# Two edge-attention layers on a graph: the prologue's order, the last three superchunks of a layer, and products added in pairs

## The chip, the cores and the metric

The kernel runs on one core of a Trainium2 chip. The metric is the time of one execution on the device in microseconds. One execution was also taken by the profiler; its page and its trace are what is read here.

## The reference

A graph has N = 6250 nodes with 256 features and E = 200,000 edges, sorted by their destination. The node features are normalised (layer norm), cut at zero, and go through two layers of graph attention; the result is added to the input. Cut to what matters (self loops with the mean of a node's edge features are added inside):

```python
h = jnp.maximum(_layernorm(x), 0.0)
def gat(x, s, d, ea, Wg, a_s, a_d, Wge, a_e, b, n, heads, f):
    hx, he = (x @ Wg).reshape(n, heads, f), (ea @ Wge).reshape(-1, heads, f)
    al = leaky_relu((hx * a_s).sum(-1)[s] + (hx * a_d).sum(-1)[d] + (he * a_e).sum(-1), 0.2)
    al = jnp.exp(al - segment_max(al, d, n)[d])
    al = al / segment_sum(al, d, n)[d]
    return segment_sum(hx[s] * al[:, :, None], d, n).reshape(n, -1) + b
te = relu(edge_attr @ We + be) * jnp.exp(x @ Wo + bo)[src][:, None]     # per layer
x1 = relu(gat(h, ..., te, 4 heads of 64) + h)
x2 = gat(x1, ..., te, 1 head of 256) + x1
out = x + x2 + h
```

## The kernel before, in words

**Tiles.** The edges are cut into 1563 chunks of 128 and these into 66 superchunks: 64 of 24 chunks, one of 14 and one of 13 (`cuts`). Each layer goes once over all superchunks, so there are 132 steps; step k is superchunk k of layer 0 for k below 66, and superchunk k - 66 of layer 1 after that. `st` holds the tiles of a step.

**The node table.** `prologue` loads x, normalises 49 tiles of 128 nodes (statistics L266 to L296, on VectorE or, for some groups, with their Newton steps on POOL; normalising L310), transposes them (L316), multiplies by the weights (L431), adds the bias (L435) and stores the rows as table T of layer 0 in DRAM. The same is done for 24 tiles of x rows gathered by source (`first_rows`, an indirect DMA each, issued by POOL at L250), which stay in the buffer G0 and so make the gathers of step 0 unnecessary. Index work of later superchunks (`index_group`) and folding the attention vectors into the weights (`fold`, `fold_e`) are woven in, one piece per tile.

**A step.** `edges` writes out the order by hand: each engine takes its instructions in the order in which the code issues them. For step k the loop issues the gathers of step k+1 (`gather` L874: one indirect DMA for each chunk, by POOL's queue, from T into one of three buffers G), the rest of the attention logits of step k (`logits`, `ends`, `links`, `maxima`), work for step k+1 (`spread`, `parts`, `rphase1`, `blocks`, `rphase2`, `adst`: edge features, and the nodes' terms brought to the edges), then `scale` (L1171: G times the weights), `carried`, `sums` (L1183: TensorE adds the scaled rows up by destination, with one-hot matrices S from `onehots` L1003), and `evict` (L1188: ScalarE copies the sums out of PSUM). `finish` of the step before (`merge`, L1204 to L1219 and what follows: self loop, division, bias, the next layer's table row) stands between `onehots` and `evict`; `rows1`, `rows2` and `rows3` make and store the rows of the nodes that are done. Superchunk s covers the nodes of a window of 112 that begins at its first destination; `nodes` loads their rows into one of five buffers `tw`.

**POOL's wait.** The gathers of a step go into a buffer that the sums of an earlier step have read, so they wait for these.

**The end of a layer.** `ending(st, nx, ...)` takes the last two superchunks together (k=64 and 65, k=130 and 131): the sums of the first are split in three with the other's work between them. At the end of layer 0 it also issues the gathers of step 66 (`after`), whose sources may lie in rows of layer 1's table that are not yet stored. The rows of the last window are therefore left out, and `add_last` (L842 to L852) adds them to the gathered rows of step 66 afterwards: 24 products of a one-hot matrix with the last 128 table rows, each followed by VectorE's addition of one chunk.

**Index data.** `index_group` fills, for a group of four superchunks, `loc`, `fpen`, `lpen`, `isl` and `pen`. `pen` is the penalty that cuts the scans of `ends` at the chunks' borders; for the four heads of layer 0 it is held in four copies (ScalarE copies three times at L604).

**Checks.** A few VectorE operations on the index data write flags into `bad`; the tile `wg`'s columns for the attention terms come from `fold`, those for the edge features from `fold_e`.

Of the kernel before, what the change touches and what calls it, by code (L numbers as in the profile page):

```python
# [31 lines left out]
P = 128  # L32
# [47 lines left out]
class Kernel:  # L80
# [32 lines left out]
    def consts(self, wp):  # L113
# [4 lines left out]
        self.wg, row, wpk = [], [], []  # L118
        self.ones = cp.tile([P, 1], F32, name="ones")
        nc.gpsimd.memset(self.ones, 1.0)  # L120
        self.bias, self.webd, self.be, wge = [], [], [], []
        for L in self.L:
            q = (nc.scalar, nc.sync)[L.l]
            wg = cp.tile([P, 2, L.MW], F32, name=f"wg{L.l}")
            q.dma_start(wg, a[f"wg{L.l}"].rearrange("(k p) m -> p k m", p=P))
            r = wp.tile([P, 3, D], F32, name=f"row{L.l}", bufs=1)
# [9 lines left out]
            e = wp.tile([P, D], F32, name=f"wge{L.l}", bufs=1)  # L136
# [34 lines left out]
        def fold(L):  # L171

            H = L.H
            for k in range(2):
                for j, c0 in ((0, L.p), (1, L.ad)):
                    t = wp.tile([P, D], F32, name="wtmp", bufs=4)
                    V.tensor_mul(t, self.wg[L.l][:, k, 0:D], row[L.l][:, j, :])
                    yield
                    V.tensor_reduce(self.wg[L.l][:, k, c0:c0 + H], t.rearrange("p (h f) -> p h f", h=H),
                                    axis=AX.X, op=OP.add)  # L180
                    yield

        def fold_e(L):

            H = L.H
            wea, we1 = self.wea[L.l]
            t = wp.tile([P, D], F32, name="wtmp", bufs=4)
            V.tensor_mul(t, wge[L.l], row[L.l][:, 2, :])
            yield
            V.tensor_reduce(we1, t.rearrange("p (h f) -> p h f", h=H), axis=AX.X, op=OP.add)  # L190
            yield
            for j in range(2):
                r = slice(j * PH, (j + 1) * PH)
                V.tensor_copy(wea[r, 32 * j:32 * j + H], we1[r, :])
            yield

        def later():
            yield from fold_e(self.L[0])
            yield from fold(self.L[1])
            yield from fold_e(self.L[1])  # L200

        return fold(self.L[0]), later()

    def prologue(self):
# [7 lines left out]
        with ExitStack() as c:  # L212
# [22 lines left out]
            for i in range(28):  # L235
                nc.tensor.matmul(warm[:, i % 2, :], self.ident, self.ident, start=True, stop=True)
# [19 lines left out]
            for _ in range(8):  # L256
                next(rows0, None)

            def stats(g):

                n, x = len(groups[g]), xs[g]
                st = wp.tile([P, GT, 6], F32, name="st", bufs=2)
                mv = wp.tile([P, GT, 2], F32, name="mv", bufs=3)
                s = wp.tile([P, 3, GT], F32, name="sc", bufs=3)
# [92 lines left out]
            for k in range(-3, len(tiles) + 1):  # L357
# [27 lines left out]
                if k >= 4:  # L385
# [19 lines left out]
    def fixed_rows(self):  # L405
# [18 lines left out]
        for i in range(2):  # L424
            self.trow1.append(cp.tile([P, 2 * L1.TW], F32, name=f"t1row{i}"))
            nc.gpsimd.memset(self.trow1[i][:, L1.TW + D:], 0.0)

# [9 lines left out]
    def indices(self, wp):  # L437
# [75 lines left out]
        chk = wp.tile([1, 9, NS + 1], F32, name="chk", bufs=1)  # L513
        V.memset(chk, 0.0)
        V.tensor_scalar(chk[:, 0, :NS], ll[0:1, :], float(M - 1), None, op0=OP.is_gt)
        V.tensor_sub(qd[0:1], qlast[0:1], qbase[0:1])
        V.tensor_scalar(chk[:, 5:9, :NS], qd[0:1], 31.0, None, op0=OP.is_gt)
        nb = wp.tile([1, NS + 1], F32, name="nb", bufs=1)
# [7 lines left out]
        V.tensor_tensor(chk[:, 3, :NS], sc0[0:1, 0, :], sc0[0:1, 2, :], op=OP.is_lt)  # L526
# [6 lines left out]
        self.before = cp.tile([P, NS], F32, name="before")  # L533
        V.tensor_copy(self.before, dpv)
        yield

    def index_tiles(self):
# [12 lines left out]
        self.pen = cp.tile([P, 4 * NCH + 1], BF, name="pen")  # L550
# [12 lines left out]
    def index_group(self, g, pool, di):  # L563
# [30 lines left out]
        pv = self.pen[:, 4 * o:4 * (o + w)].rearrange("p (s h c) -> p s h c", h=4, c=c)  # L594
# [5 lines left out]
        V.tensor_scalar(pv[:, :, 0, :], t3, 1.0, -BIG, op0=OP.min, op1=OP.mult)  # L600
        V.memset(self.pen[:, 4 * (o + w):4 * (o + w) + 1], -BIG)
        yield
        for h in range(1, 4):
            nc.scalar.activation(pv[:, :, h, :], pv[:, :, 0, :], AF.Copy)  # L604
            yield
# [11 lines left out]
    def edges(self, ctx):  # L617
# [13 lines left out]
        self.tws = [self.np_.tile([P, self.L[0].TW + D], F32, name=f"tw{i}", bufs=1) for i in range(5)]  # L631
        for t in self.tws:
            nc.vector.memset(t, 0.0)
# [11 lines left out]
        self.onehots(steps[0])  # L645
        self.edge_rows(steps[0])
# [3 lines left out]
        for k, st in enumerate(steps):  # L650
            nx = steps[k + 1] if k + 1 < len(steps) else None
            if st["s"] + 1 == self.NS:
                continue
# [4 lines left out]
            left = self.groups[self.ahead][0] - 2 - k if self.ahead < len(self.groups) else 99  # L658
# [3 lines left out]
            if st["s"] + 2 == self.NS:  # L662
                self.ending(st, nx, pv, late, steps[k + 2] if k + 2 < len(steps) else None)
# [35 lines left out]
            self.index_on(left)  # L699
            if k + 6 == self.NS:  # L700
# [12 lines left out]
    def ending(self, st, nx, pv, late, after):  # L713

        nc, k = self.nc, st["k"]
        self.load_lb(k + 3)
        self.gather(nx)
        for q in () if after else (st, nx):
# [3 lines left out]
        drain(self.logits(st))  # L722
        self.ends(st)
        self.spread(nx)
        self.parts(nx)
        y = self.rphase1(nx)
        next(y)
        self.links(st)
        if late:
            self.rows2(late)  # L730
        self.blocks(nx)
        if after:
            drain(self.finish(pv))
            self.rows3(late)
            self.rows1(pv)
            self.rows2(pv)
        drain(y)
        self.load_ea(k + 2)
        self.rphase2(nx)
        self.adst(nx)  # L740
        drain(self.maxima(st))
        if after:
            self.rows3(pv)
            self.gather(after)
            self.nodes(after)
            late = pv = None
        drain(self.scale(st))
        self.carried(st)
        c, h = nx["C"], st["C"] // 3
        self.sums(st, (0, h))  # L750
        self.edge_rows(nx)
        drain(self.logits(nx))
        self.ends(nx)
        self.sums(st, (h, 2 * h))
        self.onehots(nx)
        self.links(nx)
        self.sums(st, (2 * h, st["C"]))
        self.load_fl(k + 2)
        drain(self.maxima(nx))
        self.evict(st)  # L760
        y = self.rphase1(after) if after else iter(())
        next(y, None)
        drain(self.scale(nx, cuts=(1, 1 + c // 2, c)))
        drain(self.scale(nx, cuts=(0, 1)))
        if after:
            self.load_srow(after)
        self.carried(nx)
        self.sums(nx, (1, c), (0, 1))
        if late:
            self.rows3(late)  # L770
        if pv:
            drain(self.finish(pv))
            self.rows1(pv)
            self.rows2(pv)
            if not after:
                self.rows3(pv)
        f = self.finish(st)
        while after and "hw" not in st:
            next(f)
        if not after:  # L780
            drain(f)
            self.rows3(st)
        self.evict(nx)
        drain(f)
        drain(y)
        self.rows1(st)
        self.rows2(st)
        f = self.finish(nx)
        while after and "hw" not in nx:
            next(f)  # L790
        if after:
            self.rows3(st)
        drain(f)
        self.rows1(nx)
        self.rows2(nx)
        self.rows3(nx)
# [45 lines left out]
    def add_last(self, st):  # L842
# [5 lines left out]
        y = self.ps_y.tile([P, 1024], F32, name="y")  # L848
        for i in range(c):
            h = y[:, 512 * (i % 2):512 * (i % 2) + L.TW]  # L850
            nc.tensor.matmul(h, st["O"][:, i, :], st["last"], start=True, stop=True)
            V.tensor_add(G[:, i, 0:L.TW], G[:, i, 0:L.TW], h)  # L852
# [96 lines left out]
    def rphase1(self, st):  # L949
# [3 lines left out]
        c = st["C"]  # L953
# [98 lines left out]
    def logits(self, st):  # L1052
# [15 lines left out]
        n, p0 = H * c, 4 * o  # L1068
# [4 lines left out]
        V.tensor_tensor_scan(f, self.pen[:, p0:p0 + n], al[:, :n], -BIG, op0=OP.add, op1=OP.max)  # L1073
        yield
        V.tensor_tensor_scan(b[:, ::-1], self.pen[:, p0 + 1:p0 + n + 1][:, ::-1], al[:, :n][:, ::-1], -BIG,
# [469 lines left out]
```

## Time and profile before

| | |
|---|---|
| time before | 4817.07 us, median of 3 runs (4813.92 to 4823.6) |
| profiled execution | 4800.02 us |
| its span, first to last instruction | 4798.2 us |
| mean granted TensorE clock | 0.732 |
| busy: PE, VectorE, ScalarE, POOL | 3203.7, 2901.0, 520.2, 3011.0 us |
| first evict (k=0), first evict of layer 1 (k=66), last DMA's start | 213.2, 2623.7, 4786.9 us |

In the lines of the profile PE is TensorE's matmul, PEld its weight load, DVE VectorE, ACT ScalarE, POOL GpSimd, SP SyncE, which issues most plain DMAs. A line of the timeline has the start in us from the beginning of the span, the busy time in us, the engine, the line of the kernel, the operation, output and input tiles with their shapes, how many such instructions were put together, and in brackets the idle time of the engine just before and what ended it. A group's line (part 5 of the page) has the total busy time in us and the mean of one in ns, then the engine's idle time ahead of these instructions and its chief releaser; "issue" is time in which the engine waited for nothing that the profile shows, "remote" an event that could not be put down to an instruction.

### The profile page before, as it was taken

The numbers are of one execution on the slowest core, as the hardware profiler recorded it, in microseconds if no ns is written. First come the engines' busy times: TensorE is split into PE (matmuls) and PEld (weight loads), VectorE is DVE, ScalarE is ACT, GpSimd is POOL, SyncE is SP. The second block draws the span as 40 slices with busy tenths as digits, with TensorE's granted clock in tenths as the row PEclk, the third lists the DMA queues.
The fourth block names the chain that finished last, engine by engine and source line by source line (L and its number), as shares of the span: only waits on it lengthen the run. The fifth ranks groups of instructions, "written<-read, shape, count | busy, mean of one in ns | idle before, by whom it ended". The sixth has DMA issues, their size and how long they took to land. (4 is left out here: it accounts for less than half of the span.)

```text
span 4798.2 us, 35104 instructions
## 1 busy us (share of the span) xinstructions
PE 3203.7 (67%) x9964; PEld 1948.6 (41%) x9964; DVE 2901.0 (60%) x6782; ACT 520.2 (11%) x1152; POOL 3011.0 (63%) x3249
## 2 busy tenths in 40 slices
PE   7556766767767766767765666666666666666666
PEld 5334444444444444444442333333333433333334
DVE  6556766666766666666664555555455556455556
ACT  4111111111111111111110000000000000000000
POOL 5446666666666666666644666666666666666664
PEclk8676777776777777777775777777767777777777
DMA  6334444444444444444433444444444444444442
GB/s 218 93 104 119 128 130 119 129 131 119 130 127 122 128 128 126 124 126 127 126 108 92 126 118 117 124 120 124 116 124 126 118 116 125 119 124 117 124 125 69
DMA packets 240006, 585.82 MB, mean 122 GB/s; under 512 B 64201, under 2 KB 96655, under 8 KB 239609
## 3 DMA queue, kind: packets, MB, share of 16 engines
q0 software_dynamic: 150144, 422.75, 33.6%
q1 hardware_dynamic: 89243, 160.09, 10.2%
q8 instruction: 80, 1.31, 0.1%
q14 instruction: 123, 1.01, 0.1%
q10 hardware_dynamic: 416, 0.67, 0.0%
HBM read 544.42 MB, written 38.94 MB: 122 GB/s over the span
## 5 line engine op out<-in xcount | busy, mean ns | idle before, releaser
L874 POOL DMA_INDIRECT G<-T,src x3078 | 2937.8, 954 | 1679.3 <-issue 889.1
L1183 PE MATMUL u<-G,S 128*128 128x270 f32 (+1 forms) x6252 | 1648.0, 417 | 737.7 <-issue 588.3
L1183 PEld LDWEIGHTS u<-G,S 128*128 128x128 f32 x6252 | 1257.7, 203 | 1066.7 <-issue 643.0
L958 PE MATMUL y<-ea,webd 64*128 64x384 f32 (+1 forms) x1056 | 709.6, 795 | 326.8 <-issue 293.1
L1171 DVE TENSOR_TENSOR G<-G,kps 128x6144 f32<-128x6144 f32 (+1 forms) x137 | 853.0, 6230 | 0.0
L1096 DVE TENSOR_TENSOR_SCAN cl<-fl,cl,lf 4x129 f32<-4x129 f32 (+1 forms) x130 | 61.1, 470 | 898.5 <-remote 598.6
L958 PEld LDWEIGHTS y<-ea,webd 64*128 64x128 f32 x1056 | 281.4, 289 | 605.0 <-issue 540.2
L972 PE MATMUL zad<-R,wea 128*64 128x384 f32 (+1 forms) x1056 | 447.3, 764 | 10.2 <-ACT R L963 7.3
L1003 DVE TENSOR_TENSOR S<-kps,loc 128x3072 f32<-128x3072 f32 x132 | 437.5, 3315 | 4.5
L963 ACT ACTIVATE R<-y,webd 128x768 f32<-128x768 f32 x260 | 233.2, 897 | 649.8 <-PE y L958 293.8
L972 PEld LDWEIGHTS zad<-R,wea 128*64 128x64 f32 x1056 | 149.8, 197 | 309.5 <-issue 246.9
L1188 ACT ACTIVATE U<-u 128x270 f32<-128x270 f32 (+1 forms) x132 | 52.0, 394 | 1852.8 <-remote 1004.5
L1046 DVE STREAM_TRANSPOSE rt<-zad 128x768 f32<-128x768 f32 (+1 forms) x130 | 124.6, 959 | 15.9 <-issue 10.7
L1018 PE MATMUL zad<-a,Q 128*128 128x12 bf16 (+1 forms) x132 | 23.9, 181 | 163.4 <-issue 99.6
L431 PE MATMUL fin<-wg,h1T 128*128 128x260 f32 x264 | 119.5, 599 | 1.5 <-ACT h1T L1278 1.5
L987 DVE TENSOR_TENSOR lb<-lb,kps 128x1536 bf16<-128x1536 bf16 (+1 forms) x68 | 113.5, 1669 | 0.0
L1086 PE MATMUL lf<-ident,fb 128*36 128x128 f32 (+1 forms) x132 | 45.8, 347 | 98.6 <-issue 69.2
L431 PE MATMUL ps<-wg,hT 128*128 128x266 f32 x292 | 88.3, 429 | 28.4 <-ACT hT L318 17.8
L1103 PE MATMUL lf<-ident,cl 36*128 36x36 f32 (+1 forms) x132 | 35.4, 269 | 95.9 <-DVE cl L1098 95.8
L1270 DVE TENSOR_TENSOR t1row<-t1row,fb 128x256 f32<-128x256 f32 x66 | 28.2, 427 | 112.5 <-remote 60.4
L1103 PEld LDWEIGHTS lf<-ident,cl 36*128 36x128 f32 (+1 forms) x132 | 25.3, 192 | 168.9 <-DVE cl L1098 148.7
L1018 PEld LDWEIGHTS <-Q 128*128 128x128 bf16 x132 | 14.3, 108 | 190.7 <-issue 108.1
(202 smaller groups left out, 2248.4 us busy)
## 6 DMA issues: line engine op xcount, KB each, us to landing
G<-T,src POOLq DMA_INDIRECT x3078
ea<-in_ea_dram SPq DMA_DIRECT2D x64, 768.0 KB
lb<-locrow SPq DMA_DIRECT2D x64, 384.0 KB
T<-t1row SPq DMA_DIRECT2D x66, 227.5 KB
tw<-T SPq DMA_DIRECT2D x66, 225.8 KB
tw<-T SPq DMA_DIRECT2D x66, 117.2 KB
tw<-in_x_dram SPq DMA_DIRECT2D x66, 112.0 KB
part<-t1row SPq DMA_DIRECT2D x64, 113.8 KB
```

The source lines that it names most:

```text
L431: self.nc.tensor.matmul(ps[:, :L.MW], hT[:, k, :], self.wg[L.l][:, k, :], start=(k == 0), stop=(k == 1))
L874: nc.gpsimd.indirect_dma_start(out=G[:, c, 0:L.TW], out_offset=None, in_=rows, in_offset=bass.IndirectOffsetOnAxis(ap=idx[:, c:c + 1], axi ...
L958: nc.tensor.matmul(y[:, o], self.webd[l][r, :], ea[r, w], start=True, stop=True)
L963: nc.scalar.activation(R[:, i, :32 * c].rearrange("p (b n) -> p b n", b=2), y.rearrange("p (b n) -> p b n", b=2)[:, :, :16 * c], AF.Relu, ...
L972: nc.tensor.matmul(st["zad"][i * PH:(i + 1) * PH, o], self.wea[l][0], R[:, i, w], start=True, stop=False)
L987: V.tensor_tensor(lb[:, :, :n], lb[:, :, :n], self.k_part.unsqueeze(2).to_broadcast([P, i, n]), op=OP.is_equal)
L1003: nc.vector.tensor_tensor(st["S"][:, c0:c1, :], self.k_iota.unsqueeze(1).to_broadcast(w), self.loc[:, o + c0:o + c1].unsqueeze(2).to_broad ...
L1046: V.transpose(rv[:, :32 * c].rearrange("p (b n) -> p b n", b=2), z.rearrange("p (b n) -> p b n", b=2)[:, :, :16 * c])
L1096: V.tensor_tensor_scan(cl[:H, :], fl[:H, :], lf[:H, 0:P + 1], init, op0=OP.add, op1=OP.max)
L1103: nc.tensor.transpose(pc, cl[:n, 0:P], self.ident[0:n, 0:n])
L1171: nc.vector.tensor_tensor(v, v, pw[:, c0:c1, :].unsqueeze(3) .to_broadcast([P, c1 - c0, H, L.F]), op=OP.mult)
L1183: nc.tensor.matmul(st["u"][:, :L.W], S[:, i, :], G[:, i, 0:L.W], start=(j == 0), stop=(j == c - 1))
```

## The change

1. **Prologue.** 14 of the gathers of `first_rows` are issued ahead of the tiles (8 before); the others come one every third tile from the 15th (one every tile from the fifth before). 34 dummy matmuls on the identity come first (28 before), and 8 and 3 more at tiles 1 and 6. The statistics of the 24 gathered tiles are made in two groups of 6 and 18 (four of 6). `fold` of layer 1 moves to `edges`, behind the one-hot matrices of step 0; `fold_e` of layer 1 and the flags (`checks`) move into the loop, two pieces per step from k=6. The `tw` buffers are four, not five, and POOL zeroes them behind the 14 gathers.
2. **Penalty.** `pen` is held once; a layer-0 step copies it for its four heads into `pen4` at the start of `rphase1`, on ScalarE.
3. **Ending.** `ending(a, b, c, ...)` takes the last three superchunks (24, 14 and 13 chunks). The sums of a are split into a half and two quarters, with work of b and c between them. The step ahead of it is finished right behind its own evict.
4. **`add_last`.** Two products go to the two halves of one PSUM tile, taken in turn from two pools, and one addition takes both.

The diff, cut to these parts:

```diff
@@ prologue
-            for i in range(28):
+            for i in range(34):
                 nc.tensor.matmul(warm[:, i % 2, :], self.ident, self.ident, start=True, stop=True)
...
-            for _ in range(8):
+            for _ in range(14):
                 next(rows0, None)
+            for t in self.tws:
+                nc.gpsimd.memset(t, 0.0)
...
-            for i in range(0, CX, 6):
-                xs[len(groups)] = G0[:, i:min(i + 6, CX), 0:D]
-                groups.append(list(range(NT + i, NT + min(i + 6, CX))))
+            for i, e in ((0, min(6, CX)), (6, CX)):
+                if i < e:
+                    xs[len(groups)] = G0[:, i:e, 0:D]
+                    groups.append(list(range(NT + i, NT + e)))
...
-                    if q > g:
+                    if q > (g if k >= NT - 4 else min(g, g0)):
...
+                if k in (1, 6):
+                    idle(9 - k)
...
-                if k >= 4:
+                if k >= 14 and k % 3 == 0:
                     next(rows0, None)
@@ consts
-        def later():
-            yield from fold_e(self.L[0])
-            yield from fold(self.L[1])
-            yield from fold_e(self.L[1])
-
-        return fold(self.L[0]), later()
+        self.late, self.soon = fold_e(self.L[1]), fold(self.L[1])
+        return fold(self.L[0]), fold_e(self.L[0])
@@ index_group
-        for h in range(1, 4):
-            nc.scalar.activation(pv[:, :, h, :], pv[:, :, 0, :], AF.Copy)
-            yield
@@ rphase1
+        if H > 1:
+            st["pen"] = pen = self.pen4[st["k"] % 2]
+            nc.scalar.activation(pen[:, :H * c].rearrange("p (h c) -> p h c", c=c),
+                                 self.pen[:, o:o + c].unsqueeze(1).to_broadcast([P, H, c]), AF.Copy)
@@ nodes
-        tw = self.tws[st["k"] % 5]
+        tw = self.tws[st["k"] % 4]
@@ edges
         self.onehots(steps[0])
+        drain(self.soon)
         self.edge_rows(steps[0])
...
-            if st["s"] + 1 == self.NS:
+            if st["s"] + 2 >= self.NS:
                 continue
...
-            if st["s"] + 2 == self.NS:
-                self.ending(st, nx, pv, late, steps[k + 2] if k + 2 < len(steps) else None)
+            if st["s"] + 3 == self.NS:
+                self.ending(st, *steps[k + 1:k + 3], pv, late, steps[k + 3] if k + 3 < len(steps) else None)
...
             self.index_on(left)
+            if k >= 6:
+                next(self.late, None)
+                next(self.late, None)
+            if st["s"] + 4 == self.NS:
+                drain(self.finish(st))
@@ ending (the order of a's sums and the work between them)
+        self.gather(b)
+        self.gather(c)
...
+        drain(self.scale(a))
+        self.carried(a)
+        n = a["C"]
+        self.sums(a, (0, n // 2))
+        self.rows3(late)
+        self.edge_rows(b)
+        self.onehots(b)
+        drain(self.logits(b))
+        self.ends(b)
+        self.rows1(pv)
+        self.spread(c)
+        self.parts(c)
+        self.sums(a, (n // 2, n - n // 4))
+        self.links(b)
+        self.sums(a, (n - n // 4, n))
...
+        self.evict(a)
...
+        if after:
+            drain(self.finish(a))
+            self.rows1(a)
+            self.rows2(a)
+        drain(self.scale(b))
+        if after:
+            self.rows3(a)
+            self.gather(after)
+            self.nodes(after)
...
@@ add_last
-        y = self.ps_y.tile([P, 1024], F32, name="y")
-        for i in range(c):
-            h = y[:, 512 * (i % 2):512 * (i % 2) + L.TW]
-            nc.tensor.matmul(h, st["O"][:, i, :], st["last"], start=True, stop=True)
-            V.tensor_add(G[:, i, 0:L.TW], G[:, i, 0:L.TW], h)
+        for i in range(0, c, 2):
+            y = self.ps_y.tile([P, 1024], F32, name="y") if i % 4 else self.ps_1.tile([P, 1024], F32, name="zad")
+            n = min(2, c - i)
+            h = y.rearrange("p (j w) -> p j w", j=2)[:, :n, :L.TW]
+            for j in range(n):
+                nc.tensor.matmul(h[:, j, :], st["O"][:, i + j, :], st["last"], start=True, stop=True)
+            g = G[:, i:i + n, 0:L.TW]
+            V.tensor_add(g, g, h)
```

More of the change, by code (lines that the diff above doesn't have):

```diff
@@ L721, in ending @@
             nc.vector.memset(idx[0:1, :], 1 << 20)
[L722 to L726, printed above, removed]
-        next(y)
[L728 to L736, printed above, removed]
+        drain(self.logits(a))
+        self.ends(a)
+        self.spread(b)
@@ L751, in ending @@
[L751 to L760, printed above, removed]
+        self.carried(b)
+        m, n = c["C"], b["C"] // 3
+        self.sums(b, (0, n))
+        self.edge_rows(c)
+        drain(self.logits(c))
+        self.ends(c)
+        self.sums(b, (n, 2 * n))
+        self.onehots(c)
@@ L768, in ending @@
[L768 to L778, printed above, removed]
+        self.carried(c)
+        self.sums(c, (1, m), (0, 1))
+        if not after:
+            drain(self.finish(a))
+            self.rows3(a)
+        f = self.finish(b)
@@ L779, in ending @@
+        while after and "hw" not in b:
             next(f)
@@ L781, in ending @@
             drain(f)
[L782 to L783 removed]
+            self.rows3(b)
+        self.evict(c)
         drain(f)
         drain(y)
[L786 to L789, printed above, removed]
+        self.rows1(b)
+        self.rows2(b)
+        f = self.finish(c)
+        while after and "hw" not in c:
             next(f)
         if after:
[L792 removed]
+            self.rows3(b)
         drain(f)
[L794 to L796 removed]
+        self.rows1(c)
+        self.rows2(c)
+        self.rows3(c)
         if after:
```

119 lines of the change are left out of this document (76 added, 43 removed).

## The prediction

> **What bounds the kernel now.** I read the page first, then the timeline of POOL and ACT in one step of each layer, then the three places that the change touches: the prologue, the passage between the layers, and the end. Part 5 of the page names the two largest groups, with their idle time:
>
> ```profile
> L874 POOL DMA_INDIRECT G<-T,src x3078 | 2937.8, 954 | 1679.3 <-issue 889.1
> L1183 PE MATMUL u<-G,S 128*128 128x270 f32 (+1 forms) x6252 | 1648.0, 417 | 737.7 <-issue 588.3
> ```
>
> POOL is busy for 61% of the span and issues nearly nothing but gathers. PE's idle time is mostly "issue": it waits for no semaphore that the profile shows. The timeline of one layer-1 step says why (POOL's last gathers and its next burst, PE's starts, ACT's evict, which releases that burst):
>
> ```profile
> 3028.66 0.94 POOL L874 DMA_INDIRECT G<-T,src  x1 [0.30 <-issue]
> 3029.91 0.95 POOL L874 DMA_INDIRECT G<-T,src  x1 [0.30 <-issue]
> 3035.40 0.94 POOL L874 DMA_INDIRECT G<-T,src  x1 [4.55 <-remote]
> ...
> 3022.30 0.38 PE L1183 MATMUL u<-G,S 128*128 128x261 f32 x1 [1.31 <-issue]
> 3025.11 0.38 PE L1183 MATMUL u<-G,S 128*128 128x261 f32 x1 [2.43 <-issue]
> 3027.90 0.37 PE L1086 MATMUL lf<-ident,fb 128*33 128x128 f32 x1 [2.41 <-issue]
> ...
> 3035.17 0.39 ACT L1188 ACTIVATE U<-u 128x261 f32<-128x261 f32 x1 [18.90 <-remote]
> ```
>
> A burst is 24 gathers of 0.95 + 0.30 = 1.25 us, 30.0 us. Some 20 us into it the other engines start work only 1.3 to 2.8 us apart (I call this the crawl), and the evict comes about 4.2 us after the burst's end. 30.0 + 4.2 makes the 34.28 us step of layer 1. Layer 0 takes 35.87 us on average, its evicts 3.9 to 8.8 us behind the burst. The change leaves this cycle alone: some 120 of the 132 steps should cost what they cost, and the sum is made at the edges.
>
> The passage between the layers (k=66 is the first step of layer 1), DVE's rows of `add_last`, then POOL:
>
> ```profile
> 2558.04 0.43 DVE L852 TENSOR_TENSOR G<-G,y 128x260 f32<-128x260 f32 x1 [1.33 <-PE y L851]
> 2559.80 0.42 DVE L852 TENSOR_TENSOR G<-G,y 128x260 f32<-128x260 f32 x1 [1.33 <-PE y L851]
> 2561.55 0.43 DVE L852 TENSOR_TENSOR G<-G,y 128x260 f32<-128x260 f32 x1 [1.33 <-issue]
> 2564.85 0.42 DVE L852 TENSOR_TENSOR G<-G,y 128x260 f32<-128x260 f32 x1 [2.88 <-issue]
> 2569.75 0.43 DVE L852 TENSOR_TENSOR G<-G,y 128x260 f32<-128x260 f32 x1 [4.48 <-remote]
> ...
> 2587.42 0.95 POOL L874 DMA_INDIRECT G<-T,src  x1 [0.30 <-issue]
> 2623.89 0.95 POOL L874 DMA_INDIRECT G<-T,src  x1 [35.52 <-PE zad L1018]
> ```
>
> One product and its add take 1.75 us in turn; from 2562 on, in the crawl of a burst of 48 (2527.4 to 2588.4), 5 us. `add_last` runs from 2537.5 to 2599.9, evict(66) is at 2623.65, and POOL idles 35.5 us.
>
> **The change, part by part.** The profiled execution took 4800.0 us (span 4798.2), 17.0 below the median of the runs, 4817.1. The sum is made on the former and moved by 17.
>
> *Prologue.* The x tiles run at 1.12 us each where PE sets the pace, with stalls of 3 to 7 us at 17.4 (a crawl, to 24.3), 42.6, 57.5 (POOL's Newton steps start at 56.3, behind five gathers issued from 49.7 on) and 86 (DVE busy 18.96 of 20 us in 80 to 100). Fourteen gathers up front and one every third tile keep POOL clear for its steps; `fold(L1)`, `fold_e(L1)` and the checks leave a full DVE. Against it, the first burst of 13 gathers (5.7 to 22.0) becomes one of 14, some 1.3 us longer, with its crawl. I take the table 6 us earlier (0 to 8). Then the 24 gathered tiles take 52.7 us (93.0 to 145.7):
>
> ```profile
> 105.28 0.42 DVE L435 TENSOR_TENSOR G<-ps,bias 128x266 f32<-128x266 f32 x1
> 105.61 0.50 DVE L269 BATCH_NORM_AGGREGATE mv<-st 128x2 f32<-128x6 f32 x6
> 109.53 0.17 DVE L274 TENSOR_SCALAR sc<-mv 128x6 f32<-128x6 f32 x1 [3.42 <-remote]
> 110.91 0.17 DVE L276 TENSOR_SCALAR sc<-sc 128x6 int32<-128x6 int32 x1 [0.89 <-DVE wg L179]
> 112.30 0.17 DVE L278 TENSOR_SCALAR sc<-sc 128x6 f32<-128x6 f32 x1 [1.22 <-DVE sc L276]
> ```
>
> Eight are done by 105.3 at 1.75 us, DVE full; then the burst for k=1 (96.0 to 125.9) puts everything into a crawl until 129, small steps of the statistics standing between the tiles' adds. Two groups (6 and 18) in place of four save 30 such steps of 0.17 to 0.2 us, 6 us of DVE; the folds some 8 more in this stretch. Eight tiles at 1.12 in place of 1.75 us gain 5 us, and a few tiles more fit in before the crawl: 6 us (-3 to 14). The five `tw` memsets (2.71 us at 146.3) go to POOL as four; their cover in step 0 is its evict, which comes late in the next burst's crawl anyway, so 0. `fold(L1)`, 8 operations, 3.1 us, behind the one-hots of step 0, lies in DVE's 7 us of idleness before 162.65; 0, and 3.1 without that cover. The added dummy matmuls (6 + 8 + 3) run where PE waits for the first statistics; 0. Sum: **-12 (-22 to +3)**.
>
> *Late work.* `fold_e(L1)` and the checks, some 17 short DVE operations, come in four layer-0 steps from k=6: 17 x 0.2 = 3.4 us if none finds idle time, 8 if half of them cost a start in the crawl. I take **+3 (0 to 8)**.
>
> *pen.* Three ACT copies and one DVE memset per group of four steps go; one ACT copy per layer-0 step comes (L604, median 273 ns, is its nearest row). Its input is ready and ACT has 18.9 us idle before an evict: **0 (-5 to +5)**. *Four `tw` buffers*: SP's load for k+2 waits for finish(k-2), not (k-3), with the lb loads queued behind it; before, one was issued at 1460.3 and would now wait to 1466.9, a step (34 us) before its reader: 0.
>
> *Passage.* DVE now drains finish(62) right behind evict(62), so 5 us of finish and the logits, spread and parts queued behind it come after the evict, where they ran under the sums before: sums(63) start 7.7 us later (2456.0 for 2448.3). Weaving b's and c's work into a's sums wins about half back, so the part gathers of k=66 (2480.0 to 2509.8) and `add_last` start 4 us later, 2541.5. Twelve pairs: a product is two PE instructions, by L1183's mean 2 x 417 ns = 0.83 us, by L431 in the slow clock (four in 2.14 us at 18.94) 1.07; I take 0.88 without the handoff to DVE, whose add of some 0.75 for a pair (0.43 for one) lies beside it: 24 x 0.88 + 1 = 22 us, end 2563, not 2599.9. From the end of `add_last` to evict(66) were 23.7 us (2599.9 to 2623.65): 2587, if nothing crawled. But the 48 gathers still run to 2592.3, their crawl from about 2566 now meets scale and sums of k=66, and the evict then follows the burst: 2592.3 + 4.2, and the 10.3 us of sums (2612.9 to 2623.2) if they are still to do, some 2609. POOL starts again that much earlier. **-14**; best 2596.5 (evict straight behind the burst, -27); worst, `add_last` itself is caught by the crawl and ends at 2595: 2595 + 23.7 = 2618.7, -5.
>
> [...]
>
> *End.* finish(128) (2.95 us, as finish(127) at 4728.31 to 4731.26), the two indices, logits, spread and parts come behind evict(128): 7 to 8 us; sums(129) start at 4752.7 for 4744.95. With b and c overlapped, the idle 3.85 us before 4758.0 and the 1.42 at 4760.2 go. **+4 (-3 to +8)**.
>
> Sum: -12 + 3 + 0 - 14 + 4 = **-19**: 4781 for the profiled execution, **4798** for the median.
>
> **The rivals.** *More gain*: the crawl leaves the stages touched. It is not seen in bursts of 13 and 14 gathers (4714 to 4751), and at 2527 it took 35 us to come. Then the prologue gives -22, the passage -27, the end -3: -52, 4765. Against it: nothing shortens the bursts of 24 and 48, and an earlier start of other work may bring the crawl earlier.
>
> *POOL eats it*: the gain of `add_last` ends in the crawl (-5), the prologue's tiles, too (-6), late work and end cost 3 and 4: -4, 4813, no change. For it: POOL's work is the same, and every full burst so far has held the evict back to its end.
>
> *Slower*: the copy into `pen4`. It stands in each of 66 layer-0 steps at the head of `rphase1`, which is where y L958 and the evict run in the crawl, while the copies removed fell anywhere. Where it costs a start of 0.7 us (about the smallest spacing of starts in the crawl, all engines together) in 62 steps, it is 43 us: -19 + 43 = +24, 4841. It cancels the forecast at 19 / 62 = 0.31 us a step, and is measurably slower from 0.46 us. Against it: ACT waits at that place, and in layer 1, where no such copy is made, only the tail of 4.2 us would tell.
>
> *The change doesn't do what it says*: products in pairs stay at 1.75 us each, since DVE still reads what PE writes. Two buffers in turn speak against it; the passage then gives +4 and the sum is -1, 4816.
>
> **How the numbers follow.** Forecast (-30 to -10) 0.48, more gain 0.14, POOL eats it 0.18, pairs without effect 0.05, slower by the copy or by the early finishes without their overlap 0.15. 0.2% is 9.6 us, about the spread of the runs of before (4813.9 to 4823.6), and what can be told from no change. Faster: 0.48 + 0.14 = 0.62, less 0.01 at the forecast's edge, 0.61; same 0.18 + 0.05 = 0.23, and 0.01: 0.24; slower 0.15. Low end: the bigger gain, 4765. High end: prologue 0 (not its whole +3, since the others stand at their worst already), late work +8, passage -5, end +8, 4828. Outside lies most of the slower case, and a little of the first rival.
>
> **What would show it.** Prologue: the first gather burst for k=1 at about 90 (96.0 before), the G0 tiles ended near 133. Layer 0: evicts 35.9 us apart still; 36.2 and more is the copy. Passage: L852's successor in 12 rows, about 1.8 us apart, ended by 2563 plus the shift of the prologue; POOL's idle time before the gathers of k=69 near 17 us in place of 35.5. End: from evict(127) to the last DMA 77 us in place of 73. The prediction is wrong if the steps between move by 0.3 us, if the crawl starts sooner after a burst's start than 20 us, or if sums(63) and sums(129) start later than 8 us.

## The result, and the profile after

The changed kernel takes 4796.0 us (median of 6 runs, 4792.5 to 4799.7), the kernel before on the same chip 4820.3 us (6 runs, 4813.9 to 4825.2): 24.3 us less, a ratio of 0.9948 with an interval of 0.9938 to 0.9958. The forecast was -19 us, to 4798, and the range 4765 to 4828. The profiled execution of the changed kernel took 4792.5 us, 3.5 below its median; that of before took 4800.0, which is 20 below the median of the runs that the changed kernel is compared with. So the two profiles, held side by side, account for 7.6 us only, and a stage is compared below with the profiles of as many executions as there are. The 4800.0 us also lie below all six timed runs of that kernel (4813.9 and more); the record does not name the chip on which that profile was taken.

The steps between are what they were. POOL's last gathers of a burst, the next burst, PE's starts in the crawl and the evict, in the timeline of a layer-1 step of the changed kernel (start, busy time, engine, line, operation, tiles, idle time ahead):

```profile
2979.36 0.94 POOL L919 DMA_INDIRECT G<-T,src  x1 [0.30 <-issue]
2980.61 0.95 POOL L919 DMA_INDIRECT G<-T,src  x1 [0.30 <-issue]
2986.24 0.94 POOL L919 DMA_INDIRECT G<-T,src  x1 [4.69 <-PE zad L1070]
...
2975.94 0.59 PE L1236 MATMUL u<-G,S 128*128 128x261 f32 x1 [2.41 <-issue]
2980.83 0.60 PE L1236 MATMUL u<-G,S 128*128 128x261 f32 x1 [2.20 <-issue]
2983.63 0.37 PE L1139 MATMUL lf<-ident,fb 128*33 128x128 f32 x1 [2.20 <-issue]
...
2986.01 0.39 ACT L1241 ACTIVATE U<-u 128x261 f32<-128x261 f32 x1 [17.44 <-PE zad L1070]
```

The evict is 4.45 us behind the burst's end, the next gather 0.23 us behind the evict. Layer-1 steps are 34.28 us apart in both profiles, layer-0 steps (k=6 to 60) 35.80 before and 35.82 after.

The passage between the layers, DVE's adds of `add_last` and then POOL's first gather for k=69:

```profile
2534.93 0.70 DVE L897 TENSOR_TENSOR G<-G,zad 128x520 f32<-128x520 f32 x1 [2.21 <-PE zad L895]
2536.66 0.70 DVE L897 TENSOR_TENSOR G<-G,y 128x520 f32<-128x520 f32 x1 [1.04 <-issue]
...
2540.33 0.70 DVE L897 TENSOR_TENSOR G<-G,zad 128x520 f32<-128x520 f32 x1 [0.28 <-issue]
2541.29 0.70 DVE L897 TENSOR_TENSOR G<-G,y 128x520 f32<-128x520 f32 x1 [0.26 <-DMA G<-T,src]
...
2551.10 0.70 DVE L897 TENSOR_TENSOR G<-G,zad 128x520 f32<-128x520 f32 x1 [4.90 <-remote]
2556.73 0.70 DVE L897 TENSOR_TENSOR G<-G,y 128x520 f32<-128x520 f32 x1 [4.93 <-remote]
2565.83 0.70 DVE L897 TENSOR_TENSOR G<-G,zad 128x520 f32<-128x520 f32 x1 [8.40 <-remote]
2577.03 0.70 DVE L897 TENSOR_TENSOR G<-G,y 128x520 f32<-128x520 f32 x1 [10.50 <-issue]
...
2609.18 0.94 POOL L919 DMA_INDIRECT G<-T,src  x1 [25.63 <-PE zad L1070]
```

A pair takes 1.74 us at first and 0.97 us from 2539 on, where a single product took 1.75. But the crawl is there from about 2543, 20 us into the burst of 48, and not 35 us as before: the last four pairs take 5.6, 5.6, 9.1 and 11.2 us. In the kernel before, a single product took 5.6 us in the crawl, so in the last pair nothing of the pairing is left. From the first product (2532.8) to the end of the last add (2577.7) are 44.9 us, neither the 62.4 of before nor the 22 that were forecast. POOL's idle time falls from 35.5 to 25.6 us; the forecast was 17.

The evicts at the end, k=127, 129 and 131 of the kernel before, then k=127 to 131 of the changed one:

```profile
4714.02 0.39 ACT L1188 ACTIVATE U<-u 128x261 f32<-128x261 f32 x1 [18.13 <-remote]
4757.90 0.39 ACT L1188 ACTIVATE U<-u 128x261 f32<-128x261 f32 x1 [8.95 <-PE u L1183]
4781.63 0.37 ACT L1188 ACTIVATE U<-u 128x261 f32<-128x261 f32 x1
...
4699.77 0.39 ACT L1241 ACTIVATE U<-u 128x261 f32<-128x261 f32 x1 [17.55 <-PE zad L1070]
4721.95 0.39 ACT L1241 ACTIVATE U<-u 128x261 f32<-128x261 f32 x1 [5.21 <-PE u L1236]
4754.16 0.39 ACT L1241 ACTIVATE U<-u 128x261 f32<-128x261 f32 x1
4767.05 0.39 ACT L1241 ACTIVATE U<-u 128x261 f32<-128x261 f32 x1 [1.72 <-PE u L1236]
4773.76 0.37 ACT L1241 ACTIVATE U<-u 128x261 f32<-128x261 f32 x1
```

From the first to the last are 74.0 us (67.6 before): evict(129) comes 10.5 us later against evict(127) (54.4 against 43.9), and 4.1 of them are won back.

### The profile page after: what moved, and what is told of

Same layout as the page of the kernel before. It is cut to its first block, busy times and chain, and to the rows that moved or that the text cites. A ratio compares the mean times of both kernels' runs of the same rounds, so it can differ in the third digit from the quotient of the medians.

```text
span 4790.6 us, 35239 instructions
## 1 busy us (share of the span) xinstructions
PE 3226.4 (67%) x9998; PEld 1956.9 (41%) x9998; DVE 2896.3 (60%) x6722; ACT 524.7 (11%) x1162; POOL 3010.6 (63%) x3256
## 3 DMA queue, kind: packets, MB, share of 16 engines
q1 hardware_dynamic: 89243, 160.09, 10.2%
## 5 line engine op out<-in xcount | busy, mean ns | idle before, releaser
L1236 PEld LDWEIGHTS u<-G,S 128*128 128x128 f32 x6252 | 1245.1, 201 | 1236.9 <-issue 841.6
L1010 PE MATMUL y<-ea,webd 64*128 64x384 f32 (+1 forms) x1056 | 721.3, 822 | 191.1 <-issue 135.9
L1024 PE MATMUL zad<-R,wea 128*64 128x384 f32 (+1 forms) x1056 | 458.6, 784 | 9.0 <-ACT R L1015 7.5
L1323 DVE TENSOR_TENSOR t1row<-t1row,fb 128x256 f32<-128x256 f32 x66 | 28.1, 425 | 119.4 <-remote 43.9
L1139 PEld LDWEIGHTS lf<-ident,fb 128*36 128x36 f32 (+1 forms) x132 | 16.7, 126 | 189.2 <-issue 104.4
L1070 PEld LDWEIGHTS <-Q 128*128 128x128 bf16 x132 | 14.5, 110 | 192.3 <-issue 109.6
L439 PEld LDWEIGHTS fin<-wg,h1T 128*128 128x128 f32 x264 | 70.5, 295 | 46.0 <-issue 32.1
```

What stands on the lines that cost most here:

```text
L439: self.nc.tensor.matmul(ps[:, :L.MW], hT[:, k, :], self.wg[L.l][:, k, :], start=(k == 0), stop=(k == 1))
L1010: nc.tensor.matmul(y[:, o], self.webd[l][r, :], ea[r, w], start=True, stop=True)
L1024: nc.tensor.matmul(st["zad"][i * PH:(i + 1) * PH, o], self.wea[l][0], R[:, i, w], start=True, stop=False)
L1139: self.nc.tensor.transpose(self.lf[0:e.shape[1], 1:P + 1], e, self.ident)
L1236: nc.tensor.matmul(st["u"][:, :L.W], S[:, i, :], G[:, i, 0:L.W], start=(j == 0), stop=(j == c - 1))
```

## The experiments

They fall into three groups (the expectations say calls), each on a chip of its own beside the kernel before. On the first of these chips that kernel takes 4801 us; on the other two 4058 and 4060 us. There the crawl is missing, as the second group will show, so a time is compared only with others of its own chip. The ratios are those on record, with their 95% intervals; differences in us are between medians, so the two agree only roughly.

**First group: the parts, with the crawl.** The kernel before again; before with the new `add_last`; the changed kernel with the old one; and the changed kernel with the old `ending`.

```diff
 b_pairs: before.py, add_last as in the change;  a_singles: after.py, add_last as before
-        for i in range(c):
-            h = y[:, 512 * (i % 2):512 * (i % 2) + L.TW]
+        for i in range(0, c, 2):
...
 a_oldend: after.py
-            if st["s"] + 4 == self.NS:
-                drain(self.finish(st))
...
-    def ending(self, a, b, c, pv, late, after):
+    def ending(self, st, nx, pv, late, after):
```

> The kernel before, unchanged, for a second profile of it. Its profiled execution was 17 us under the median of its timed ones (4800.0 against 4817 to 4820), the changed kernel's only 3.6 under (4792.5 against 4796.0). Theory: the time between executions differs in layer 0, whose steps are 34.3 or 36 to 39 us long, so this profile's layer-0 evicts are on average 36.0 us apart (35.80 in the first profile) and the prologue, the passage between the layers and the end lie within 2 us of the first. Rival: the passage or the prologue differs from one execution to the next, by 10 us or more, and layer 0 does not. Ratio to before 1.000 by both.

> Before, with the pairs of add_last alone. Theory (add_last 62.4 us before, 45 in the changed kernel, but the burst of 48 gathers holds what comes behind it to its own end): evict(66) 10 us earlier than before, time -10 (0.998). Rival, POOL eats it: evict(66) at most 3 us earlier, ratio 0.9995 or more. Prediction's own term: -18 here (ends at 2609 without the 4 us of the early finish).

> The changed kernel with single products in add_last. Theory: 10 us slower than the changed kernel (0.997 of before), add_last some 62 us long again. Rival, POOL eats it: as the changed kernel, 0.995.

> The changed kernel with the ending over two superchunks and no early finish. Theory (the ending over three costs 6 us at the end, and some at the passage, since its evicts 63 and 129 come 13 and 10 us later against their neighbours): 6 to 12 us faster than the changed kernel, 0.993 of before, and from evict(127) to the last DMA 73 us, not 79. Rival (overlap of the last superchunks pays): slower than the changed kernel by 3 us or more.

Before again: 4799.2 us, ratio 1.0002 (0.9993 to 1.0012). Pairs alone: 4791.3, ratio 0.9980 (0.9971 to 0.9989), 10.2 us less. All but the pairs: 4797.6, ratio 0.9995 (0.9986 to 1.0004), 3.8 us less. All but the ending: 4777.4, ratio 0.9954 (0.9941 to 0.9968), 24.1 us less. The stages in the profiles, in us (evict(0) and evict(5) from the start of the span, the others from one evict to another; the part gathers are the 24 gathers `G<-part,pidx` that begin the burst of 48):

| kernel | evict(0) | evict(5) | evict(5) to (60) | evict(62) to part gathers | evict(62) to (66) | POOL idle before k=69 | evict(127) to (131) |
|---|---|---|---|---|---|---|---|
| before | 213.2 | 403.8 | 1968.8 | 43.0 | 186.7 | 35.5 | 67.6 |
| b_again | 214.1 | 400.1 | 1965.7 | 43.1 | 186.8 | 35.6 | 68.0 |
| b_pairs | 214.7 | 404.7 | 1970.1 | 43.3 | 177.0 | 25.7 | 68.0 |
| changed | 191.0 | 391.7 | 1970.3 | 50.8 | 184.5 | 25.6 | 74.0 |
| a_singles | 193.6 | 394.6 | 1964.9 | 50.8 | 196.1 | 37.1 | 74.8 |
| a_oldend | 192.5 | 393.3 | 1966.8 | 46.7 | 180.5 | 25.6 | 68.2 |

The three profiles with the old prologue and the three with the new one agree with each other to 5.4 us and better up to evict(60). The pairs are worth 9.7 us in the kernel before and 11.6 in the changed one, which decides for "10 us" against "POOL eats it". The prologue is worth 9.7 us at evict(5) (402.9 against 393.2 on average). The ending over three superchunks costs with the crawl: 9.3 us at the passage without pairs (196.1 against before's 186.8), 4.0 or 7.5 with them (against a_oldend, b_pairs), and 6.4 us at the end (74.4 against 68.0 on average). Whether the kernel with the old ending beats the changed one, as expected, by 6 to 12 us cannot be said here, since the changed kernel was not run on this chip; its ratio of 0.9954 is not the 0.993 of that theory. The first theory on before is not borne out: its second profile has the same stages, layer 0 no slower, and its runs on this chip (4799 and 4801 us) are where the first profile was, so nothing is left here for the theory to explain.

**Second group: the ending's early finish, and the first crawl.** The prologue of the changed kernel showed a thing that the forecast had not. PE's timeline from 5 us on (a dummy product is two instructions, and the 53 are those of the 34 products' 68 that lie in this window; then the first tile's transposes, the second's):

```profile
4.72 6.55 PE L237 MATMUL pT<-ident 128*128 128x128 f32 x53
11.37 0.44 PE L321 MATMUL pT<-ident,h 128*128 128x128 f32 x2
20.89 0.66 PE L321 MATMUL pT<-ident,h 128*128 128x128 f32 x2 [9.09 <-remote]
```

PE stands for 9 us in the crawl of the 14 gathers, and the first table row is kept at 25.8 us (28.2 and 28.3 in the other two profiles with the new prologue, 16.7 to 23.4 in the three with the old one). TensorE's granted clock is 1.00 from 5.7 to 15.9 us there, 0.50 to 26.2 us, and 1.00 again behind that.

```diff
 a_latefin: after.py
-            if st["s"] + 4 == self.NS:
-                drain(self.finish(st))
...
         self.onehots(b)
+        drain(self.finish(pv))
 a_fewwarm: after.py
-            for i in range(34):
+            for i in range(6):
 a_8first: after.py
-            for _ in range(14):
+            for _ in range(8):
...
-                if k >= 14 and k % 3 == 0:
+                if k >= 8 and k % 2 == 0:
```

> The changed kernel, unchanged, beside the others of this call and with a second profile. Adding up the profiles of the first call against those of before: prologue -11, passage between the layers -2, end +6, so 7 us faster than before on this chip: ratio 0.9985. Rival (the first measurement of the change, 0.9948, holds on every chip): 25 us faster.

> The changed kernel, with finish(62) and finish(128) behind onehots(b) of the ending, not right behind their own evict. Theory (the early finish is what puts sums(63) and sums(129) off, and the part gathers behind them by 7.7 us): evict(63) 33 us behind evict(62) in place of 37.5, part gathers for k=66 5 us sooner, from evict(127) to evict(131) 70 us in place of 74; 8 us faster than the changed kernel. Rival (the finish only changes places with other work of VectorE that the same evicts wait for, the three-way order itself is what costs): within 2 us of the changed kernel.

> The changed kernel with 6 dummy matmuls in front, not 34. In its profile TensorE's first transposes wait 9 us (11.4 to 20.9) in the crawl of the 14 gathers. Theory (a burst leaves the other engines some 100 to 200 starts before they crawl, dummies counted): 56 starts fewer let the first tiles through, the first table row is kept at 14 to 18 us, not 23 to 28, and G0 is done 3 to 8 us sooner. Rival (the crawl comes a fixed time after the first gather): the transposes still wait until 21, and the time is the same or, with a cold clock, 2 us longer.

> The changed kernel with 8 gathers in front of the tiles and 16 after them, one every second tile from the ninth, not 14 and one every third. Theory (the 14 make the first crawl last until 24): first table row near 17 us, the table's last store some 6 us sooner, evict(5) 5 us sooner than in the changed kernel, ratio better by 0.001. Rival (the later gathers take it back: POOL's steps stand behind them as before, at 57 us): same time.

On this chip before takes 4057.8 us. The changed kernel: 4037.0, ratio 0.9949 (0.9936 to 0.9963). Late finish: 4043.5, 0.9960 (0.9947 to 0.9974). Few dummies: 4038.1, 0.9952 (0.9937 to 0.9968). Eight gathers first: 4038.4, 0.9954 (0.9938 to 0.9969). The profile of the changed kernel has its evicts 30.03 us apart in both layers, and the first table row is kept at 16.6 us with 34 or 6 dummies, 14 or 8 gathers. Of the two theories on the changed kernel the ratio of the first measurement held (0.9949); the adding up of the stages was made for the crawl and is not tested where there is none. So what the last two were to tell apart does not occur here, and they are inconclusive on the crawl; what they show is that without it neither number matters.

Late finish goes against the theory of 8 us faster: its median is 6.5 us above the changed kernel's. Four of its five runs (4041.9 to 4044.8) lie above all thirteen of the other three versions on this chip (4036.5 to 4040.3), the fifth (4037.5) among them, and the intervals overlap. Its evict(63) is 43.7 us behind evict(62), that of the other three 37.0 to 40.7, and POOL stands 23.4 us before the part gathers, 18.6 in the changed kernel. There finish(62) lies in VectorE's queue ahead of the logits, spread and parts of b and c, and PE's second half of sums(63) is queued behind the products of `parts(c)` that wait for these. That chain is read from the order of the code. That the early finish is not the worse place of the two is measured without the crawl; with it, neither place was compared.

**Third group: before, the change, the old ending and late `tw` on one chip.**

```diff
 a_oldend2: as a_oldend
 a_twlate: after.py
-            for t in self.tws:
-                nc.gpsimd.memset(t, 0.0)
...
         self.state = {0: None, 1: None}
+        for t in self.tws:
+            nc.vector.memset(t, 0.0)
```

> The kernel before, unchanged, for a profile beside the others of this call. In the second call the chip showed no crawl at all: evicts 30.0 us apart in both layers for the changed kernel, POOL gathering without a break from 83.0 on, and yet the same ratio of 0.9949. If this chip is such a one: first burst near 92 (the table 9 us later), add_last 43 us (24 singles of 1.75), passage and prologue together 20 us and more longer than in the changed kernel, the end 10 us shorter. If it is one with the crawl: as the two profiles of before that there are, within 6 us at each stage.

> The changed kernel, unchanged, beside a_oldend2 on one chip. With the crawl or without: 0.995 of before.

> The changed kernel with the ending over two superchunks and no early finish, again, beside the changed kernel on one chip. Theory (the ending over three costs: 4 to 9 us at the passage and 6 at the end in the profiles of the first call): with the crawl 10 us faster than the changed kernel, 0.993 of before; without it, where the first call says nothing, the end of before may be shorter by more. Rival (the chips differ and the three-way overlap pays where nothing crawls): the same or up to 10 us slower than the changed kernel.

> The changed kernel with the four tw buffers zeroed by VectorE in edges, as before, so that the loads of the first tw follow behind the prologue. Theory (of the prologue's 10 us, which the prediction put into the table and the gathered tiles, most comes in step 0, where the changed kernel needs 28 us from the last gathered tile to sums(0) and before 38): with the crawl evict(0) 10 us and evict(5) 3 to 8 us later than in the changed kernel; without the crawl POOL has the next bursts anyway, evict(5) within 1 us and the time the same. Rival (the 10 us come of fold and the checks taken out of that stretch): evict(0) at most 4 us later.

Before takes 4059.7 us here, its copy 1.0003 of that (0.9993 to 1.0012). The changed kernel: 4041.4, ratio 0.9956 (0.9943 to 0.9970). Old ending: 4039.2, 0.9951 (0.9938 to 0.9965). Late `tw`: 4041.6, 0.9955 (0.9941 to 0.9968). The chip is again one without the crawl. POOL's rows of the kernel before, then of the changed one: the first gather from the table, the part gathers, and (before alone) the gather for k=69:

```profile
89.12 1.07 POOL L874 DMA_INDIRECT G<-T,src  x1 [18.21 <-ACT hT L318]
...
2047.92 0.94 POOL L874 DMA_INDIRECT G<-part,pidx  x1 [14.42 <-DVE G L1161]
...
2154.76 0.94 POOL L874 DMA_INDIRECT G<-T,src  x1 [14.55 <-PE zad L1018]
```

```profile
82.67 0.94 POOL L919 DMA_INDIRECT G<-T,src  x1 [11.96 <-issue]
...
2042.49 0.94 POOL L919 DMA_INDIRECT G<-part,pidx  x1 [17.25 <-DVE al L1118]
```

Without the crawl POOL waits for no evict in the changed kernel and for one in the kernel before (the 14.55 us, which evict(66) at 2154.53 ends), and the time is its first gather, its gathers, and its few pauses. The changed kernel starts 6.5 us sooner, and the pause of 14.55 us behind `add_last` is gone; the pauses of 2 us and more behind the first gather, those at the end included, sum to 53.9 us before and 38.5 after. 6.5 + 15.4 = 21.9 us; the spans differ by 21.8 (4061.4, 4039.6). With the old ending the pauses are 38.1 us: the ending over three superchunks makes no difference here that can be told. Two adds of single products in the kernel before, then the changed kernel's pairs, which run as they were meant to:

```profile
2097.13 0.42 DVE L852 TENSOR_TENSOR G<-G,y 128x260 f32<-128x260 f32 x1 [1.33 <-PE y L851]
2098.88 0.43 DVE L852 TENSOR_TENSOR G<-G,y 128x260 f32<-128x260 f32 x1 [1.33 <-PE y L851]
...
2087.53 0.70 DVE L897 TENSOR_TENSOR G<-G,y 128x520 f32<-128x520 f32 x1 [0.18 <-PE y L895]
2088.58 0.70 DVE L897 TENSOR_TENSOR G<-G,zad 128x520 f32<-128x520 f32 x1 [0.36 <-PE zad L895]
2089.46 0.70 DVE L897 TENSOR_TENSOR G<-G,y 128x520 f32<-128x520 f32 x1 [0.18 <-PE y L895]
```

About 0.97 us a pair, DVE busy for 0.70 of it: 14.7 us from the first product (2079.4) to the end of the last add (2094.0), against 42.0 us (2088.8 to 2130.9) in the kernel before on this chip, 1.75 us a product.

Late `tw` puts evict(0) 5.1 us and evict(5) 2.6 us later (152.6 for 147.5, 281.1 for 278.5), and the whole time is the same, as the theory said for a chip without the crawl, if with 2.6 us for "within 1". From the last gathered tile to sums(0) it takes 32.3 us, the changed kernel 29.0 and the kernel before 32.6: without the crawl nearly all that step 0 gains is the early `tw` (with its zeroing off VectorE). The theory's other half, 10 us at evict(0) with the crawl, was not measured.

## Why the prediction was right, point by point

**The sum** was -19 and the measurement -24.3. The terms did not come out as well as their sum: the stages in the profiles give -9.7, -2.2 and +6.4 us where the forecast had -12, -14 and +4, in all -5.5. That -19 came so near -24.3 is thus not explained by its terms, and as far as these runs show it is in part luck.

**The prologue, -12**: 9.7 us at evict(5), the size right, the working wrong. It had the table 6 us earlier and the gathered tiles 6 us shorter. With the crawl, the first gather from the table starts at 95.1 us before and at 94.9 after (means of three), and the last gathered tile is kept at 144.3 and 145.9: neither gained. The step that failed is the crawl of the first burst, priced at "some 1.3 us longer": it now catches the very first tile (the 9 us above), and what the tiles win after it (stalls at 42, 57 and 86) only makes that good. Whether the added gather or the added dummy products brought it there no run shows, since a_8first and a_fewwarm met no crawl. The gain lies behind the last gathered tile, in step 0, which the sum held at nothing, and step 1: POOL's second burst starts 1.5 us later than before (146.6 against 145.1, means of three), its third 3.9 us earlier (180.7 against 184.6), its fourth, which waits for the sums of step 1, 9.4 us earlier (220.1 against 229.5). The last gathered tile, the first use of `tw` and sums(0) in the kernel before, then DVE's rows from the last gathered tile to the transposed logits, and sums(0), in the changed one:

```profile
145.30 0.43 DVE L435 TENSOR_TENSOR G<-ps,bias 128x266 f32<-128x266 f32 x1 [0.46 <-PE ps L431]
150.87 0.17 DVE L1013 CAST a<-tw 128x4 bf16<-128x4 f32 x1
184.29 11.75 PE L1183 MATMUL u<-G,S 128*128 128x270 f32 x48
...
144.04 0.43 DVE L443 TENSOR_TENSOR G<-ps,bias 128x266 f32<-128x266 f32 x1 [0.46 <-PE ps L439]
146.62 0.37 DVE L1065 CAST a<-tw 128x4 bf16<-128x4 f32 x1
148.17 3.36 DVE L1055 TENSOR_TENSOR S<-kps,loc 128x3072 f32<-128x3072 f32 x1
151.44 0.42 DVE L178 TENSOR_TENSOR wtmp<-wg,row 128x256 f32<-128x256 f32 x1
157.08 0.98 DVE L1098 STREAM_TRANSPOSE rt<-zad 128x768 f32<-128x768 f32 x1 [2.41 <-PE zad L1084]
172.66 11.26 PE L1236 MATMUL u<-G,S 128*128 128x270 f32 x48
```

The `tw` rows are there at 146.6 us (their loads were issued from 91.9 on) instead of behind five memsets at 150.9, `fold(L1)` fills a pause as forecast (151.4 to 154.7), and sums(0) start 28.6 us behind the last gathered tile (172.7; 29.9 and 30.2 in the other two profiles); before, 39.0 us (145.3 to 184.3) in all three. On the chip without the crawl it is as the sum had it: the first gather from the table 6.5 us earlier (89.1 to 82.7), and the last gathered tile kept at 107.3 us in place of 117.6. How much of the 9 to 10 us in step 0 with the crawl is the early `tw` was not settled, since a_twlate met no crawl; without it, it is 3.2 of 3.5 us.

**Late work +3, pen 0**: evict(5) to evict(60) is 1968.2 us on average before, 1967.3 after. Both cost nothing that can be seen, and the slower rival, 0.31 us a step and more for the copy into `pen4`, is out: it would be 17 us here.

**The passage, -14**: 2.2 us by the two profiles. The pairs gave 10 (18 by the forecast's own rows, which the early ending was to cut to 14). The step that failed is that the crawl starts at a time, "from about 2566": it started at 2543. It is the pairs that brought it forward: the last add on time starts 34.2 us into the burst in all three profiles with single products, the one with the new ending among them, and 16.5 to 18.6 us into it in the three with pairs. So here a stage made faster meets the crawl sooner. In the kernel before, the other engines had made some 115 starts in the 34.7 us from the burst's start to the crawl, in the changed one some 105 in 20.4 us (waits and DMA issues of their sequencers counted). That the count is what decides is consistent with these two and not shown, as five bursts looked at within the layers have 170 to 200. The second failing term is the ending: the part gathers were to start 4 us later, since half of the 7.7 us would be won back; sums(63) start 21.1 us behind evict(62) in place of 11.4, 9.7 us later and more than the 8 that the prediction named as a sign of being wrong (sums(129) with 7.4 stay below it); the part gathers start 7.8 us later (50.8 against 43.0). The weaving wins back most at evict(64), 2.4 us late (57.4 against 55.0), but POOL's burst has begun late by then, and evict(65), which follows it, is 7.7 us late (84.6 against 76.9).

In the pairs TensorE's granted clock rises: from 0.50 to 1.00 at 2538.4 us, 5.6 us after the first product (at 2084.4 us and 5.0 us on the chip without the crawl, where the adds stand 1.73 us apart at first and 0.88 and 1.05 in turn from 2084.7 on); from 2548.6, in the crawl, it is 0.50 again. With single products it is 0.50 all through (2537.5 to 2599.9 in the kernel before); the slow clock of the forecast's row at 18.94 us is 0.50 too. Without the crawl `add_last` then takes 14.7 us, less than the 22 of the forecast; with it the pairs ran at 0.97 us only from 2539 to about 2542.

**The end, +4**: +6.4 (74.0 against 67.6), within the bounds; evict(129) came 10.5 us late and not 7 to 8, and the two pauses won back 4.1 of the 5.3 us that were put on them. Without the crawl the end is neither better nor worse (82.1 to 83.5 us with the ending over three, 83.3 and 84.1 with the old one).

**The rivals.** More gain: its condition, no crawl, holds on two of the chips for the whole kernel, and there the change brings 18 to 21 us, not the 52 of that rival but 0.995 all the same, because POOL's gathers run without a pause and only its start and its pauses count. POOL eats it: half true, POOL's idle time before k=69 falls by 10 us and not by the 18 that pairs alone were to give. The changed kernel without the ending over three is not slower anywhere (0.9954 and 0.9951, where the change itself has 0.9948, 0.9949 and 0.9956), but they met on one chip only, where their intervals overlap; so no version is shown to beat the changed kernel.

**Open**: how the -24.3 us divide on the chip of the first comparison. The stages in the profiles give 5.5 us in all and the two whole profiles 7.6; the differences of whole times in the first group give 10.2 for the pairs and 13.9 for the prologue (24.1 - 10.2), with the ending at +10 (13.9 - 3.8). By these the change would be worth 14 us with the crawl; the changed kernel itself was not run on that chip.

## What to carry to other kernels

Find what the stages in between are paced by (here POOL's bursts) and price an edge of the kernel in that engine's idle time: `add_last` shortened by 17.5 us with the crawl and by 27 us without was worth the 10 and 14.5 us by which POOL's pause shrank. Look at the first consumer of a buffer prepared late, even one of a few microseconds such as `tw` here: what sits between two stages shows in neither. And interleaving more steps at an end has to be measured by itself: here it cost with the crawl and changed nothing without.

## What the runs showed of the hardware

The same kernel takes 4801 us on one chip, 4820 on the chip of the first comparison, and 4058 and 4060 on two others, because on the latter two the other engines do not slow down while POOL issues indirect gathers. In the crawl of a layer-1 step with it (2974 to 2985 us of the changed kernel) the starts of all other engines together come 0.70 or 1.40 us apart. Between 2700 and 3900 us three profiles with the crawl (before, changed, b_again) have 381 to 395 such spacings, to 0.03 us, and three without it (a_again, a_third, b_third) 1 to 3. Two evicts of the changed kernel on a chip without it, one layer-1 step apart (29.3 us here, 30.1 on average):

```profile
3007.71 0.39 ACT L1241 ACTIVATE U<-u 128x261 f32<-128x261 f32 x1 [5.21 <-PE u L1236]
3037.05 0.39 ACT L1241 ACTIVATE U<-u 128x261 f32<-128x261 f32 x1 [5.22 <-PE u L1236]
```

With the crawl the layer-1 step is the burst of 30.0 us and 4.2 more; without it, the burst alone. What makes the engines crawl on some chips and not on others was not found.
